# Moving the exactness flag's product forward, a hint on the branch behind it, and a branch body without GpSimd DMAs

## The chip, the cores and the metric

The kernel runs on one core of one Trainium2 chip. The metric is device time in microseconds. It includes a little of what lies around the program, so it is slightly longer than the span from the program's first recorded instruction to its last.

## What is computed

The input is eight images of 384 channels and 32 x 32 pixels. Two blocks follow each other, in float32.

```python
# block 0: a transformer layer on the 1024 tokens of each image
xn = layernorm(xf, g1, beta1)
q, k, v = split(einsum('bnc,oc->bno', xn, w_qkv) + b_qkv)      # 8 heads of 48
attn = softmax(einsum('bhnd,bhmd->bhnm', q, k) * SCALE)
x1 = einsum('bnc,oc->bno', heads(attn @ v), w_proj) + b_proj + xf
h = gelu(einsum('bnc,oc->bno', layernorm(x1, g2, beta2), w_fc1) + b_fc1)
y = x1 + einsum('bnh,oh->bno', h, w_fc2) + b_fc2
# block 1: a convolution block with a global response norm
z = depthwise_conv7x7(y, dw_w) + dw_b
h = gelu((layernorm(z) * ln_w + ln_b) @ w1 + b1)              # 384 -> 1536
gx = sqrt(sum(h * h, pixels)); nx = gx / (mean(gx, channels) + eps)
out = y + (gamma * (h * nx) + beta + h) @ w2 + b2              # 1536 -> 384
```

## The kernel before, in words

The whole work is unrolled over the images in a function `main()` (L1500 to 1671). Channels lie on the 128 partitions, in three groups; pixels lie along the free dimension. TensorE does the products of image b while VectorE does the depthwise convolution of another image, ScalarE the exponentials and gelus, and GpSimd some adding DMAs. The order of the instructions on each engine is the order in which the code issues them (`tc.manual_schedule`, L1674). Chains of VectorE and ScalarE work are woven in between products by a small planner, `Flow`, which adds up estimated TensorE time and steps a chain when its time has come. [...]

The softmax of `main()` does not subtract a row maximum. So the kernel has a second way of computing everything, `exact_path()` (L1677 to 1700), which does subtract it, in a loop over the images. Which way counts is decided from the smallest and largest sum of exponentials, `low` and `high`, which `rest()` inside `attention` updates for each image:

- L1704 to 1706: `fine` is 1 on each partition where `low` and `high` lie within bounds. Three VectorE instructions. They stand behind `main()` in the code, but not under its fixed order, and the trace has them at 2903 us, during the attention of the last image.
- L1708: a product with a matrix of ones adds `fine` over the partitions into a PSUM tile `n_fine`.
- L1710: VectorE compares the sum with 127.5 and writes `again`, an integer.
- L1712: `values_load` makes every one of the five engines read `again` from SBUF into a register.
- L1713: every engine compares and branches. With the inputs used here `again` is 0, and the exact path is skipped.

In the program as built, the body of the exact path stands between the branch and the block that is jumped to. On GpSimd some 90 instructions lie in between, on SP 230, on ScalarE 580, on VectorE 700 and on TensorE 5,100. The block that is jumped to has only bookkeeping: each engine raises its semaphores by as much as the exact path would have raised them. ScalarE, VectorE and TensorE do that in one instruction each, SP in eight (one for each DMA semaphore). GpSimd does it in one, `INC_SWDGE_SEM`, for the eight semaphores of its own DMAs, behind four waits. Then follows the end of the program (under L1800): twelve waits of SP for all semaphores, and two barriers, in which every engine drains, reports, and is released by GpSimd.

The last work of `main()` is the product with w2 of the last image, `grn_down_straight` (L1110 to 1140): nine blocks of 12 products each (L1130), each followed by one VectorE addition (L1138) and one output DMA on SP's queue (L1139). Ahead of it stand the last block of the same product for the image before (L1668) and the end of `grn_scale` (L1669), which has a small product with ones of its own (`gxsum`, L1188) and scales the first weights of w2.

Of the kernel before, what the change touches and what calls it, by code (L numbers as in the profile page):

```python
# [46 lines left out]
F32 = mybir.dt.float32  # L47
AF = mybir.ActivationFunctionType
ALU = mybir.AluOpType
AX = mybir.AxisListType  # L50

P = 128
# [99 lines left out]
def block_kernel(  # L152
# [13 lines left out]
    nc = tc.nc  # L166
# [10 lines left out]
    ps_o = ctx.enter_context(tc.tile_pool(name="ps_o", bufs=4, space=PSUM))  # L177
    flow = Flow()
    quiet = []
    s_fc2 = dram.tile([P, len(FORMS), 4 * P], F32, tag="s_fc2", bufs=1, name="s_fc2")  # L180
    s_w2 = dram.tile([P, len(FORMS), 4 * P], F32, tag="s_w2", bufs=1, name="s_w2")
    s_qk = dram.tile([P, CT, 4 * P], F32, tag="s_qk", bufs=1, name="s_qk")
# [52 lines left out]
    def o_tile(name):  # L235
        return ps_o.tile([P, NH], F32, tag="o", name=name)
# [551 lines left out]

    def difference(dst, more, less):

        nc.scalar.mul(dst, less, -1.0)
        nc.gpsimd.dma_start(out=dst, in_=more, accum_op=ALU.add)

# [34 lines left out]
    def by_thirds(xt, hid, e, made, weights, wname, column, done, name):  # L828

        b11, b12, b21, b22, b31, b32 = (
            [hid[:, 4 * k + 2 * i : 4 * k + 2 * i + 2, half(n)] for i in range(2)] for k in range(3) for n in range(2)
        )
        c11, c12, c21, c22, c31, c32 = (xt[:, r, half(n)] for r in range(CT) for n in range(2))
        spare = three.tile([P, 2, NH], F32, tag="p", name=f"{name}_spare")
        count = iter(range(len(FORMS)))

        def product(pairs):  # L840
            n = next(count)
            if n % 2:
                bank = ps_s.tile([P, 2, NH], F32, tag="s", name=f"{name}_p{n}")[:, 0, :]
            else:
                bank = o_tile(f"{name}_p{n}")
            w = weights.at(wname, n)
            accumulate(bank, [(w[:, k, :], pairs[k // 2][:, k % 2, :]) for k in range(4)])
            weights.used(wname, n)
            return bank

        def copy(dst, bank):
            nc.scalar.copy(dst, bank)
            return dst

        def temporary(key):
            return two.tile([P, NH], F32, tag="r", name=f"{name}_{key}")

        def bias(r, dst, part):
            nc.vector.scalar_tensor_tensor(dst, part, column(r), dst, ALU.add, ALU.add)

        def op(dst, x, y, which=ALU.add):
            nc.vector.tensor_tensor(dst, x, y, which)  # L862

        def both_pairs(dst, x, y, which=ALU.add):
            for i in range(2):
                op(dst[i], x[i], y[i], which)
                yield 1.6

        def adding(dst, src):
            for i in range(2):  # L870
                nc.gpsimd.dma_start(out=dst[i], in_=src[i], accum_op=ALU.add)

        making_e = None if made else flow.spawn(both_pairs(e, b11, b12, ALU.subtract), paced=True)
        n16 = copy(spare[:, 0, :], product(b12))
        bias(2, c31, product(b21))
        flow.finish(making_e)
        f, h = b21, b11
        making_f = flow.spawn(both_pairs(f, e, b21, ALU.subtract), paced=True)
        making_h = flow.spawn(after(making_f, both_pairs(h, e, b31, ALU.subtract)), paced=True)
        p = product(e)  # L880
        making_e = flow.spawn(after(making_h, both_pairs(e, h, b12)), paced=True)
        op(c31, p, c31)
        op(c21, c21, p, ALU.subtract)
        bias(2, c32, product(b22))
        flow.finish(making_f)
        g = b22
        adding(g, f)
        n17 = copy(spare[:, 1, :], product(f))
        flow.finish(making_h)
        n15 = copy(temporary("n15"), product(h))  # L890
        flow.finish(making_e)
        adding(h, b32)
        p = product(e)
        op(n15, p, n15)
        flow.finish(flow.spawn(both_pairs(f, f, b12)))
        bias(0, c11, p)
        bias(0, c12, n15)
        op(n16, n15, n16)
        op(c32, n16, c32)
        op(n17, n16, n17)  # L900
        op(c31, n17, c31)
        done(2, 0)
        bias(1, c22, product(g))
        adding(g, b32)
        op(c11, product(b31), c11)
        op(n17, product(f), n17, ALU.subtract)
        making_f = flow.spawn(after(None, both_pairs(f, f, g, ALU.subtract)), paced=True)
        d = b31
        making_d = flow.spawn(after(making_f, both_pairs(d, g, b31, ALU.subtract)), paced=True)
        p = product(h)  # L910
        op(c12, p, c12)
        op(c22, c22, p, ALU.subtract)
        op(c32, p, c32)
        done(2, 1)
        n18 = copy(temporary("n18"), product(g))
        flow.finish(making_f)
        p = product(f)
        op(n18, p, n18)
        op(c12, p, c12)
        op(c11, n18, c11)  # L920
        op(n17, n18, n17)
        op(c22, n17, c22)
        done(1, 1)
        bias(1, c21, n17)
        op(c12, product(b32), c12)
        done(0, 1)
        flow.finish(making_d)
        p = product(d)
        op(c11, p, c11)
        done(0, 0)  # L930
        op(c21, p, c21)
        done(1, 0)
# [26 lines left out]
    def keep(b, xt):  # L959

        kept = dram.tile([C, N], F32, tag="kept", name=f"kept_{b}")
        nc.sync.dma_start(out=kept.rearrange("(c p) n -> p c n", p=P), in_=xt)
        return kept
# [475 lines left out]
    def first_values(xn):  # L1439
# [45 lines left out]
        for what in FIRST.split():  # L1485
# [11 lines left out]
            else:  # L1497
                step(what)

    def main():  # L1500
        nc.gpsimd.memset(ones, 1.0)
        nc.gpsimd.memset(eps0, EPS0)
# [105 lines left out]
        for b in range(B):  # L1608
# [6 lines left out]
            if b < B - 1:  # L1615
                mlp(b, xt, xn, weights, b, ln2, rest, lambda: next_norms(b), lambda ln: conv_norm(b, ln))
            else:
                acc = state["acc"]
                mlp_by_halves(b, xt, xn, weights, ln2, rest, last_convolution)
            kept[b] = keep(b, xt)  # L1620
            if b + 1 < B:
                acc = state["acc"]
# [45 lines left out]
        grn_down_straight(*args, f"{B - 2}_b", B - 2, blocks[-1:])  # L1668
        flow.finish(scale)  # L1669
        blocks = [(r, part) for r in range(CT) for part in LAST]  # L1670
        grn_down_straight(B - 1, y_last, kept[B - 1], weights, B - 1, B - 1, blocks)

    engines = {nc.tensor.engine, nc.vector.engine, nc.scalar.engine, nc.gpsimd.engine, nc.sync.engine}
    with tc.manual_schedule(engines=engines):  # L1674
        main()

    def exact_path():  # L1677

        load_wqkv(nc.scalar, nc.scalar)
        with tc.For_i(0, B) as b:  # L1680
            table[0] = None
            weights = Weights(plan_fc1("x") + plan_fc2_fast("x") + plan_w1("x") + plan_w2("x"))
            xn, xt = load_x(b, "xn"), load_x(b, "x")
            flow.finish(both(xn, xn, eps0, "g1", "ln1_x", True))
            values("x", xn)
            qT, kT, last_tile, _ = qk("x", xn)
            last_tile()
            exact_attention(xt, qT, kT)
            xn = one.tile([P, CT, N], F32, tag="xn", name="xn2_x")
            flow.finish(layernorm(xt, xn, 0, eps0, "g2", "ln2_x", True))  # L1690
            ln = layernorm(xt, xn, 1, eps0, "g2", "ln2_x", True)
            mlp("x", xt, xn, weights, "x", ln, None)
            kept = keep("x", xt)
            acc = one.tile([P, CT, N], F32, tag="acc", name="acc_x")
            flow.finish(convolution(acc, 0))
            flow.finish(both(acc, acc, eps1, "lnw", "ln3_x", True))
            flow.finish(block_differences(acc))
            y, gx = grn_up("x", acc, weights, "x")
            flow.finish(grn_scale("x", gx, weights, "x", y))
            grn_down("x", y, load_kept("x", kept), weights, "x", b)  # L1700


    fine = small.tile([P, 2], F32, tag="fine", name="fine")
    nc.vector.tensor_scalar(fine[:, 0:1], low, SUM_LOW, None, ALU.is_ge)  # L1704
    nc.vector.tensor_scalar(fine[:, 1:2], high, SUM_HIGH, None, ALU.is_le)
    nc.vector.tensor_tensor(fine[:, 0:1], fine[:, 0:1], fine[:, 1:2], ALU.mult)
    ps = o_tile("n_fine")
    nc.tensor.matmul(out=ps[:, :1], lhsT=ones, rhs=fine[:, 0:1], start=True, stop=True)  # L1708
    again = small.tile([P, 1], mybir.dt.int32, tag="again", name="again")
    nc.vector.tensor_scalar(again, ps[:, :1], P - 0.5, None, ALU.is_lt)  # L1710
    skip = "a comparison gives 0 or 1"
    seen = nc.values_load(again[0:1, 0:1], min_val=0, max_val=1, skip_runtime_bounds_check_because=skip)  # L1712
    with tc.If(seen > 0):  # L1713
        exact_path()


# [87 lines left out]
```

## Time and profile before

| what | us |
|---|---|
| three runs: median (lowest to highest) | 3299.46 (3298.49 to 3303.13) |
| the profiled execution's own time | 3299.18 |
| its span, first to last instruction | 3297.2 |
| TensorE busy in the span | 3274.5 (99%) |
| VectorE, ScalarE, GpSimd busy | 2392.0, 1604.5, 484.2 |
| span from the last product's start (L1708) to the end | 11.3 |

How to read it: the time outside the span (3299.18 - 3297.2 = 2.0 us) is what the program doesn't record. A "q" behind an engine's name means its instruction queue: branches, waits, register loads and DMA issues, which do not count as busy time. L1713 is line 1713 of the kernel. A group such as "x8: 17/17/17" gives the number of instructions and the shortest, median and longest duration in ns, and after it the start of the first and of the last, in us.

### The profile page before, as it was taken

What the parts mean: (1) busy time and instruction counts of PE and PEld (TensorE: products, weight loads), DVE (VectorE), ACT (ScalarE), POOL (GpSimd) and SP (SyncE); (2) the same over time, 40 slices, a digit from 0 to 9 for tenths busy, and PEclk for the clock granted to TensorE, in tenths of its full rate; (3) what the DMA queues carried; (4) which work ended last, traced back from release to release, by engine and by line L of the source; (5) the groups of instructions that cost most, each with busy time, mean ns of one, the idle gap of its engine ahead of it and who ended that gap; (6) DMA issues with size and microseconds to landing.
All of it is one profiled execution on the core that took longest, in us unless ns stands there. A gap on an engine that the chain in (4) does not pass through costs nothing.

```text
span 3297.2 us, 38818 instructions
## 1 busy us (share of the span) xinstructions
PE 3274.5 (99%) x14330; PEld 1418.3 (43%) x14330; DVE 2392.0 (73%) x3178; ACT 1604.5 (49%) x2194; POOL 484.2 (15%) x569
## 2 busy tenths in 40 slices
PE   9999999999999999999999999999999999999998
PEld 5344444443344433444344443444434444444455
DVE  4445787887857978579786797767876788879840
ACT  3542663447534375353662636526474355623541
POOL 2111210112110121101111022110220112100000
PEclk9999999999999999999999999999999999999999
DMA  5336732657244663537436374273842647333231
GB/s 198 116 107 153 149 61 71 160 115 151 54 105 134 142 124 57 132 105 173 86 58 146 103 182 76 53 168 92 183 73 58 179 92 172 69 79 89 69 96 43
DMA packets 199110, 368.74 MB, mean 112 GB/s; under 512 B 40768, under 2 KB 46784, under 8 KB 198528
## 3 DMA queue, kind: packets, MB, share of 16 engines
q0 software_dynamic: 80896, 158.63, 26.4%
q1 hardware_dynamic: 117728, 206.83, 20.8%
q8 instruction: 116, 1.90, 0.2%
q10 hardware_dynamic: 288, 0.71, 0.1%
q14 instruction: 82, 0.67, 0.1%
HBM read 187.03 MB, written 34.60 MB: 67 GB/s over the span
## 4 chain that ended last, share of the span: by engine, by line
PE 98%; DVE 1%; DMA 1%; ACT 0%; issue 0%; POOL 0%; SPq 0%; DVEq 0%; POOLq 0%; ACTq 0%
PE fc L351 17%; PE s L670 13%; PE o L690 13%; PE h L358 10%; PE fc_p L358 10%; PE o_p L358 9%; PE qk L358 6%; PE v L590 4%; PE o L1130 4%; PE proj L612 4%; PE h_last L1174 2%; PE h L338 2%; PE qk L338 1%; PE ln_sum L394 1%; PE ln_var L394 1%; PE ln_var L380 0%
## 5 line engine op out<-in xcount | busy, mean ns | idle before, releaser
L1004 DVE SCALAR_TENSOR_TENSOR acc<-pad,vec,acc 128x870 f32<-128x870 f32 (+7 forms) x861 | 963.3, 1154 | 9.1 <-DMA acc<-tap 4.5
L679 ACT ACTIVATE p<-s 128x1024 f32<-128x1024 f32 x512 | 524.0, 1024 | 283.6 <-PE s L670 276.6
L670 PE MATMUL s<-qk 48*64 48x512 f32 x4096 | 541.5, 592 | 0.2 <-ACT qk L505 0.2
L690 PE MATMUL o<-p,v 64*64 64x512 f32 x4096 | 537.7, 589 | 0.0
L351 PE MATMUL fc<-xn,fc 128*128 128x512 f32 x1152 | 502.3, 594 | 0.0
L1026 POOL DMA_DIRECT2D acc<-tap x294 | 253.5, 884 | 1208.9 <-ACT tap L1025 751.4
L351 PEld LDWEIGHTS fc<-xn,fc 128*128 128x128 f32 x1152 | 217.5, 190 | 280.6 <-issue 269.3
L358 PE MATMUL fc_p<-hid,fc 128*128 128x512 f32 x728 | 317.7, 593 | 0.0
L370 ACT ACTIVATE hid<-fc,bfc_f 128x512 f32<-128x512 f32 x192 | 131.3, 686 | 344.3 <-PE fc L351 344.2
L690 PEld LDWEIGHTS o<-p,v 64*64 64x64 f32 x4096 | 163.5, 133 | 278.4 <-issue 270.2
L670 PEld LDWEIGHTS s<-qk 48*64 48x64 f32 x4096 | 159.7, 133 | 277.2 <-issue 221.8
L358 PE MATMUL o_p<-y,w 128*128 128x512 f32 x624 | 270.9, 592 | 0.0
L1075 DVE TENSOR_TENSOR y<-h,y 128x512 f32<-128x512 f32 x288 | 196.7, 689 | 90.0 <-PE h L358 75.4
L1025 ACT ACTIVATE tap<-pad,vec 128x512 f32<-128x512 f32 x294 | 213.0, 734 | 18.6 <-DMA acc<-tap 18.4
L358 PEld LDWEIGHTS fc_p<-hid,fc 128*128 128x128 f32 x728 | 137.7, 190 | 176.5 <-issue 172.4
L358 PE MATMUL h<-acc,w_A 128*128 128x512 f32 x432 | 207.2, 595 | 0.0
L358 PEld LDWEIGHTS o_p<-y,w 128*128 128x128 f32 x624 | 118.0, 190 | 148.7 <-issue 132.0
L1004 DVE SCALAR_TENSOR_TENSOR wqkv<-pad,vec,wqkv 128x377 f32<-128x377 f32 (+24 forms) x288 | 177.2, 684 | 0.6
L631 DVE TENSOR_TENSOR attn<-o,attn 128x512 f32<-128x512 f32 x64 | 44.1, 689 | 166.9 <-ACT attn L629 166.9
L796 ACT COPY pad<-x 128x512 f32<-128x512 f32 x48 | 30.2, 635 | 247.6 <-DVE x L862 191.7
L549 DVE TENSOR_TENSOR qk<-qk,qk 128x512 f32<-128x512 f32 x168 | 114.3, 688 | 37.4 <-PE qk L358 26.9
L612 PE MATMUL proj<-attn,wproj_sb 128*128 128x512 f32 x288 | 127.3, 595 | 0.5 <-DVE attn L657 0.5
(334 smaller groups left out, 3754.2 us busy)
## 6 DMA issues: line engine op xcount, KB each, us to landing
acc<-tap POOLq DMA_DIRECT2D x294, 256.0 KB, 3.5
w_A<-in_w SPq DMA_DIRECT2D x72, 384.0 KB
fc<-s_fc SPq DMA_DIRECT2D x91, 256.0 KB
hid<-hid POOLq DMA_DIRECT2D x42, 512.0 KB, 6.9
fc<-in_wfc SPq DMA_DIRECT2D x54, 384.0 KB
w<-s_w SPq DMA_DIRECT2D x78, 256.0 KB
y<-y POOLq DMA_DIRECT2D x36, 512.0 KB, 7.0
kept<-x SPq DMA_DIRECT2D x8, 1536.0 KB
```

Source lines behind the costliest of these rows:

```text
L351: nc.tensor.matmul(out=ps, lhsT=lhsT(k), rhs=rhs(k)[:, half(h)], start=(k == 0), stop=(k == nk - 1))
L358: nc.tensor.matmul(out=bank, lhsT=lhsT, rhs=rhs, start=k == 0, stop=k == len(pairs) - 1)
L590: nc.tensor.matmul(out=ps[:, :C], lhsT=xn[:, k, t * P : (t + 1) * P], rhs=wv_sb[:, k, :], start=(k == 0), stop=(k == CT - 1),)
L612: nc.tensor.matmul(out=ps, lhsT=wproj_sb[:, m, ct * P : (ct + 1) * P], rhs=attn[:, m, :], start=(m == 0), stop=(m == CT - 1),)
L670: nc.tensor.matmul(out=s[64 * i : 64 * i + 64, j, :], lhsT=kT[64 * j : 64 * j + HD, m, k0 : k0 + 64], rhs=qT[64 * j : 64 * j + HD, m, half ...
L679: nc.scalar.activation(p, s, AF.Exp)
L690: nc.tensor.matmul(out=outs[i][64 * j : 64 * j + 64, :], lhsT=v[keys, t, at : at + 64], rhs=p[keys, j, :], start=(t == 0), stop=(t == KT - 1),
L1004: nc.vector.scalar_tensor_tensor(dst, window, tap, dst, ALU.mult, ALU.add)
L1025: nc.scalar.mul(t.rearrange("p (h w) -> p h w", w=W), window, tap)
L1026: nc.gpsimd.dma_start(out=acc[:, ct, half(h)], in_=t, accum_op=ALU.add)
L1075: nc.vector.tensor_tensor(dst, bank, part, ALU.add)
L1130: nc.tensor.matmul(out=ps, lhsT=tiles[k], rhs=y(k, part), start=(k == 0), stop=(k == HT - 1))
```

## The change

Three things are changed.

1. In `exact_path()` nothing is issued on GpSimd's DMA queue any more: a Python flag `exact[0]` is set while it is recorded, and then `difference` and `adding`, which make two differences and twelve sums by adding DMAs for each image, use VectorE instructions instead. `main()` is recorded before the flag is set and is not touched by that.
2. The flag is computed inside `main()`: `fine` behind the MLP of the last image, the product with ones and `again` directly ahead of the last image's `grn_down_straight`. What is left behind `main()` is the register load and the branch.
3. The branch gets a label, and a hint "LikelyTaken" for it is placed ahead of `main()` on all five engines. In the built program it is one instruction on each engine, behind the entry barrier and ahead of everything else of `main()`; it names the branch. The jump over the exact path is the branch's taken side.

```diff
+    exact = [False]
...
     def difference(dst, more, less):
 
+        if exact[0]:
+            nc.vector.tensor_tensor(dst, more, less, ALU.subtract)
+            return
         nc.scalar.mul(dst, less, -1.0)
         nc.gpsimd.dma_start(out=dst, in_=more, accum_op=ALU.add)
...
         def adding(dst, src):
             for i in range(2):
-                nc.gpsimd.dma_start(out=dst[i], in_=src[i], accum_op=ALU.add)
+                if exact[0]:
+                    op(dst[i], dst[i], src[i])
+                else:
+                    nc.gpsimd.dma_start(out=dst[i], in_=src[i], accum_op=ALU.add)
...
+    def whether_fine():
+
+        fine = small.tile([P, 2], F32, tag="fine", name="fine")
+        nc.vector.tensor_scalar(fine[:, 0:1], low, SUM_LOW, None, ALU.is_ge)
+        nc.vector.tensor_scalar(fine[:, 1:2], high, SUM_HIGH, None, ALU.is_le)
+        nc.vector.tensor_tensor(fine[:, 0:1], fine[:, 0:1], fine[:, 1:2], ALU.mult)
+        return fine
+
+    def whether_again(fine):
+
+        ps = o_tile("n_fine")
+        nc.tensor.matmul(out=ps[:, :1], lhsT=ones, rhs=fine[:, 0:1], start=True, stop=True)
+        again = small.tile([P, 1], mybir.dt.int32, tag="again", name="again")
+        nc.vector.tensor_scalar(again, ps[:, :1], P - 0.5, None, ALU.is_lt)
+        return again
...
                 mlp_by_halves(b, xt, xn, weights, ln2, rest, last_convolution)
+                fine = whether_fine()
...
         blocks = [(r, part) for r in range(CT) for part in LAST]
+        again = whether_again(fine)
         grn_down_straight(B - 1, y_last, kept[B - 1], weights, B - 1, B - 1, blocks)
+        return again
 
+    tc.mark_branch_hint_location("exact", "LikelyTaken", engines)
     with tc.manual_schedule(engines=engines):
-        main()
+        again = main()
 
     def exact_path():
 
+        exact[0] = True
...
-    fine = small.tile([P, 2], F32, tag="fine", name="fine")
-    nc.vector.tensor_scalar(fine[:, 0:1], low, SUM_LOW, None, ALU.is_ge)
-    nc.vector.tensor_scalar(fine[:, 1:2], high, SUM_HIGH, None, ALU.is_le)
-    nc.vector.tensor_tensor(fine[:, 0:1], fine[:, 0:1], fine[:, 1:2], ALU.mult)
-    ps = o_tile("n_fine")
-    nc.tensor.matmul(out=ps[:, :1], lhsT=ones, rhs=fine[:, 0:1], start=True, stop=True)
-    again = small.tile([P, 1], mybir.dt.int32, tag="again", name="again")
-    nc.vector.tensor_scalar(again, ps[:, :1], P - 0.5, None, ALU.is_lt)
     skip = "a comparison gives 0 or 1"
     seen = nc.values_load(again[0:1, 0:1], min_val=0, max_val=1, skip_runtime_bounds_check_because=skip)
-    with tc.If(seen > 0):
+    with tc.If(seen > 0, label="exact"):
         exact_path()
```

More of the change, by code (lines that the diff above doesn't have):

```diff
@@ L1498, in first_values @@
                 step(what)
+    def whether_fine():
[10 more added lines that the diff above has]
+        return again
+    engines = {nc.tensor.engine, nc.vector.engine, nc.scalar.engine, nc.gpsimd.engine, nc.sync.engine}
     def main():
@@ L1670, in main @@
         blocks = [(r, part) for r in range(CT) for part in LAST]
+        again = whether_again(fine)
         grn_down_straight(B - 1, y_last, kept[B - 1], weights, B - 1, B - 1, blocks)
-    engines = {nc.tensor.engine, nc.vector.engine, nc.scalar.engine, nc.gpsimd.engine, nc.sync.engine}
+        return again
+    tc.mark_branch_hint_location("exact", "LikelyTaken", engines)
     with tc.manual_schedule(engines=engines):
-        main()
+        again = main()
     def exact_path():
+        exact[0] = True
         load_wqkv(nc.scalar, nc.scalar)
```

## The prediction

> **What bounds the kernel now.** I read the page first, then the chain of work that ended last, then what each engine did behind the last product.
>
> ```profile
> span 3297.2 us, 38818 instructions
> ...
> PE 3274.5 (99%) x14330; PEld 1418.3 (43%) x14330; DVE 2392.0 (73%) x3178; ACT 1604.5 (49%) x2194; POOL 484.2 (15%) x569
> ...
> q8 instruction: 116, 1.90, 0.2%
> ...
> q14 instruction: 82, 0.67, 0.1%
> ...
> PE 98%; DVE 1%; DMA 1%; ACT 0%; issue 0%; POOL 0%; SPq 0%; DVEq 0%; POOLq 0%; ACTq 0%
> ```
>
> TensorE is busy 99% of the span and makes 98% of the chain, and the change leaves its products alone. So only the tail can gain. The two "instruction" queues are the fetches of the program itself: 116 packets of 16.4 KB (1.90 MB / 116) and 82 of 8.2 KB (0.67 MB / 82). The chain in the last 17 us:
>
> ```profile
> 3279.95 6.21 PE o L1130 x23
> 3286.16 0.02 issue
> 3286.18 0.55 DVE res L1138
> 3286.74 0.06 DVE again L1710
> ```
>
> It stops at 3286.8, and the span ends at 3297.2: 10.4 us without any busy engine. The last output DMA is issued on SP at 3286.764 (L1139), and all engines read the flag from 3286.8 to 3287.7 (L1712, 0.46 to 0.54 us each). What follows is in the groups of two lines of the kernel, the branch and the end of the program:
>
> ```profile
> L1713 SPq EVENT_SEMAPHORE  x8: 17/17/17, 3290.9 to 3291.4; - x8
> ...
> L1713 POOLq COMPARE_BRANCH  x1: 45/45/45, 3287.4 to 3287.4; - x1
> L1713 PEldq COMPARE_BRANCH  x1: 3809/3809/3809, 3287.4 to 3287.4; - x1
> L1713 DVEq COMPARE_BRANCH  x1: 72/72/72, 3287.4 to 3287.4; - x1
> L1713 SPq COMPARE_BRANCH  x1: 50/50/50, 3287.8 to 3287.8; - x1
> L1713 POOLq INC_SWDGE_SEM  x1: 1797/1797/1797, 3287.9 to 3287.9; - x1
> L1713 ACTq EVENT_SEMAPHORE  x1: 17/17/17, 3290.7 to 3290.7; - x1
> L1713 DVEq EVENT_SEMAPHORE  x1: 21/21/21, 3290.9 to 3290.9; - x1
> L1713 PEldq EVENT_SEMAPHORE  x1: 51/51/51, 3291.3 to 3291.3; - x1
> ```
>
> ```profile
> L1800 POOLq DRAIN  x3: 51/107/6679, 3289.7 to 3297.0; - x3
> L1800 SPq DRAIN  x3: 7/7/13, 3292.2 to 3296.7; - x3
> L1800 PEldq DRAIN  x2: 8/8/8, 3291.4 to 3296.7; - x2
> L1800 DVEq DRAIN  x2: 10/64/117, 3293.6 to 3296.7; - x2
> ```
>
> Two things are to be seen. First, the jump: PE, ACT, DVE and SP stand 3.1 to 3.8 us between branch and next instruction (SP: 3287.751 to 3290.872), GpSimd only 0.19 (3287.398 to 3287.586). Second, GpSimd: `INC_SWDGE_SEM` takes 1.8 us and the drain behind it 6.68, to 3296.418; all others have drained by 3292.3 (SP) and 3293.7 (DVE) and wait for it. GpSimd's drain sets the end, and 0.83 us of barriers follow (to 3297.247).
>
> [...]packets on the instruction queues at 3288.5 to 3288.8, 1.1 us after the branches, and the engines go on 2.2 us later; GpSimd, whose target is 90 instructions away, goes on at once. [...]here 45 to 72 ns are recorded where no fetch is in it. [...]the last output landed at 3288.573 by its semaphore, 1.81 us after its issue at 3286.764 (the one before: 1.84). [...]
>
> **The change part by part.**
>
> *The exact path without GpSimd DMAs.* The jumped-to block of GpSimd loses its four waits and `INC_SWDGE_SEM`. A drain of GpSimd elsewhere takes 0.05 to 0.19 us (other rows of that group, 0.186 at the entry). Alone, this moves the last drain from 3296.4 to DVE's at 3293.69: 2.7 us. DVE's own drain is late because, between 3290.9 and 3293.6, it waits for a second fetch (packet at 3291.4)[...].
>
> *The flag ahead.* `n_fine` costs PE what `gxsum` costs in the chain, 0.12 us for its two passes, now in front of the last w2 instead of behind it: +0.12. Its operands are old by then. On DVE `again` (0.146) goes between two additions that lie 7 us apart, and the three instructions of `fine` (0.46 us) move from 2903 to about 3026; the DVE queue waits 3.7, 1.1, 1.3 and 1.5 us for PE later on, so they cost nothing; without that cover they would cost 0.5. Behind the last product no engine waits for `again` any more. GpSimd, which has no work in the last stretch, and ACT, whose last activation ends at 3230.7, take their branch some 55 us before the end: load, fetch, `INC_SWDGE_SEM` and drain would all be hidden there. So for GpSimd the first two edits remove the same stall; it counts once. PE and DVE come to the branch at about 3286.6 and 3286.9 instead of 3287.4. SP doesn't: its register load stood behind the last DMA's issue already. What is queued behind SP's load is only the end.
>
> *The hint.* It adds one instruction to each engine ahead of everything. On SP it stands before the first load of x, with which the chain begins. No hint runs in the trace before. Its cost there lies between 0 and 0.2 us: register moves at the entry stand 0.07 us apart on SP; I take 0.07. Its gain lies between nothing and the whole stall, down to GpSimd's 0.19 us: SP 2.9 us. I take the whole; the stalls of PE (to 3290.6 then) and DVE (3290.4) matter only if they stay.
>
> *The sum, hint working.* Last output issued at 3286.764 + 0.07 + 0.12 = 3286.95; landed 1.81 later, 3288.76. SP has jumped at 3288.15 and stands at the second of its eight waits, for this DMA. From there to its drain's report it took 3290.967 to 3292.297 = 1.33 us: 3290.09, with 0.02 to wake up 3290.11. PE, DVE, ACT and GpSimd are long there. Barriers 0.83: 3290.94. That is 6.3 us less than 3297.247. The profiled execution took 3299.18, so 3292.9; the median of the runs is 0.28 higher: **3293.2**. The new last wait is SP's, for the output, and its row of semaphore instructions.
>
> **The rivals.**
>
> *A, the hint works on every engine: 3293.2.* [...]Its own range is 3292.0 to 3294.6: both small shifts may be 0 (-0.2), start and product dearer (+0.4), a wait in DVE's or PE's jump may remain in part, and the three runs before spread by some us.
>
> *B, the hint does nothing at its branch*[...]. SP stalls as before: 3292.297 + 0.19 for its report, 0.02, 0.83: 3293.34, a gain of 3.9: 3295.5. PE and DVE are done by 3290.7. For it: nothing in the profile shows a hint that survives fetches.
>
> *C, the hint fetches at once* [...]one extra stall of 2.2 to 3.8 us on PE or SP in the first 30 us, where PE has no slack: 3293.2 + 3.3 = 3296.5.
>
> *D, slower: [...]* PE crosses some 114 blocks of 16.4 KB. If each crossing fetched the jump's target in place of the next block, it would cost about 2.2 us each, 250 us: 3543. It decides from (6.3 + 6.6) / 114 = 0.11 us for each block on. Against it: a block lasts PE some 29 us and a fetch of one takes 0.9 to 1.0[...].
>
> *The change may also not do what it says:* the 6.7 us may be GpSimd's drain itself and not `INC_SWDGE_SEM`. The time would be A's all the same, since the drain then lies at 3225.
>
> **How the numbers follow.** A 0.70, B 0.20, C 0.04, D 0.06. The measurement of this kernel tells 0.2% (6.6 us, below 3292.86 or above 3306.1) from no change. A lies 0.3 us on the near side of the lower bound, less than its unknowns; I split it 0.38 below and 0.32 above, leaning lower because the last output no longer lands among four fetches. So faster 0.38, same 0.32 + 0.20 + 0.04 = 0.56, slower 0.06. The range goes from 3291.0 (A's lower end and a median 1 us low) to 3296.8 (B and most of C); D and the far end of each case are left out.
>
> **What would show it.** The register loads of GpSimd and ACT at 3225 and 3231; no `INC_SWDGE_SEM` at the end; branch to next instruction 0.2 us on PE, DVE and SP (A) or 3.1 to 3.8 (B); a packet on the instruction queues for each target long before 3286 (A) or 1.1 us after the branch (B); SP's drain last, near 3290.1. C would show as a gap on PE within the first 30 us, D as a gap on PE at each packet of q8. I would be wrong if another engine than SP reports last, or if the time outside the span isn't 2.0 us any more.

## The result and the profile after

| | before | changed |
|---|---|---|
| median of 22 runs each, us | 3299.98 | 3295.64 |
| ratio, 95% interval | | 0.9986, 0.998 to 0.9993 |
| the profiled execution's own time | 3299.18 | 3294.61 |
| its span | 3297.2 | 3292.8 |
| last output's DMA issued on SP | 3286.76 | 3288.60 |
| from there to the end of the span (the tail) | 10.48 | 4.23 |

The kernel is 4.3 us faster by the medians, and 2.3 to 6.6 us by the interval (0.0007 and 0.002 of 3300): a real gain, but one within 0.2%. Two runs of the changed kernel, of 3437.91 and 18366.36 us, stand apart from its other twenty and are not in the ratio.

The page of the changed kernel, its lines for the span, the engines, the instruction queues and the chain:

```profile
span 3292.8 us, 38818 instructions
...
PE 3275.4 (99%) x14330; PEld 1415.7 (43%) x14330; DVE 2393.0 (73%) x3178; ACT 1605.6 (49%) x2194; POOL 484.5 (15%) x569
...
q8 instruction: 115, 1.88, 0.2%
...
q14 instruction: 77, 0.63, 0.1%
...
PE 89%; DVE 1%; DMA 0%; issue 0%; ACT 0%; SPq 0%; POOL 0%; DVEq 0%; POOLq 0%
```

The engines do what they did before. The instruction queues carry one packet less (q8, 115 for 116) and five less (q14, 77 for 82). That PE's share of the chain is 89% and not 98% says nothing of the kernel: here the chain is followed back only to 308.5 us. Its last pieces, in order of time (start, us, what):

```profile
3274.66 13.34 PE o L1137 x51
3288.00 0.03 issue
3288.03 0.55 DVE res L1145
```

As before, the chain stops with the last addition; `again` is no longer behind it. Next the two lines of the kernel that made the tail before. First the branch (now L1734), as groups of instructions:

```profile
L1734 SPq EVENT_SEMAPHORE  x8: 17/17/17, 3290.1 to 3291.1; - x8
L1734 POOLq COMPARE_BRANCH  x1: 65/65/65, 3227.2 to 3227.2; - x1
L1734 ACTq COMPARE_BRANCH  x1: 68/68/68, 3229.4 to 3229.4; - x1
L1734 ACTq EVENT_SEMAPHORE  x1: 17/17/17, 3232.3 to 3232.3; - x1
L1734 PEldq COMPARE_BRANCH  x1: 504/504/504, 3283.6 to 3283.6; - x1
L1734 PEldq EVENT_SEMAPHORE  x1: 51/51/51, 3288.0 to 3288.0; - x1
L1734 DVEq COMPARE_BRANCH  x1: 84/84/84, 3288.6 to 3288.6; - x1
L1734 DVEq EVENT_SEMAPHORE  x1: 21/21/21, 3289.2 to 3289.2; - x1
L1734 SPq COMPARE_BRANCH  x1: 70/70/70, 3289.6 to 3289.6; - x1
```

GpSimd and ACT branch 66 and 63 us before the end. (ACT's queue goes on 2.9 us after its branch, although it has the hint: until 3232.29 its own last activations run, which stand ahead of the branch in the code.) VectorE and SP go on 0.59 and 0.51 us after their branch (3288.649 to 3289.237, 3289.595 to 3290.109), where it was over 3 us. PE's branch itself takes 0.504 us, where it took 3.809; it comes 5.0 us ahead of the last output's issue, and PE's products go on beside it. `INC_SWDGE_SEM` is gone. Then the end of the program (L1821), which has the entry's hints as well:

```profile
L1821 POOLq DRAIN  x3: 51/103/6685, 3227.4 to 3292.6; - x3
L1821 SPq DRAIN  x3: 7/7/13, 3291.9 to 3292.3; - x3
...
L1821 PEldq DRAIN  x2: 8/8/8, 3288.2 to 3292.3; - x2
L1821 DVEq DRAIN  x2: 10/14/17, 3289.3 to 3292.3; - x2
...
L1821 SPq BRANCH_PREFETCH_HINT  x1: 56/56/56, 0.8 to 0.8; - x1
```

The line to read is the first. GpSimd's long drain is still there, with 6,685 ns, and it begins at 3227.4, with no `INC_SWDGE_SEM` ahead of it. It was not removed, it was moved under PE's work. SP drains last now, at 3291.9; DVE has drained 2.6 us before.

### The profile page after: what moved, and what is told of

Read it like the earlier page. It is cut to its first block, busy times and chain, and to the rows that moved or that the text cites. A ratio compares the mean times of both kernels' runs of the same rounds, so it can differ in the third digit from the quotient of the medians.

```text
span 3292.8 us, 38818 instructions
## 1 busy us (share of the span) xinstructions
PE 3275.4 (99%) x14330; PEld 1415.7 (43%) x14330; DVE 2393.0 (73%) x3178; ACT 1605.6 (49%) x2194; POOL 484.5 (15%) x569
## 4 chain that ended last, share of the span: by engine, by line
PE 89%; DVE 1%; DMA 0%; issue 0%; ACT 0%; SPq 0%; POOL 0%; DVEq 0%; POOLq 0%
PE fc L352 15%; PE s L671 12%; PE o L691 12%; PE h L359 10%; PE fc_p L359 10%; PE o_p L359 9%; PE qk L359 6%; PE o L1137 4%; PE v L591 3%; PE proj L613 3%; PE h_last L1181 2%; PE h L339 2%; PE ln_var L395 1%; PE ln_sum L395 1%; PE ln_var L381 0%; PE ln_sum L381 0%
## 5 line engine op out<-in xcount | busy, mean ns | idle before, releaser
L1082 DVE TENSOR_TENSOR y<-h,y 128x512 f32<-128x512 f32 x288 | 197.0, 690 | 89.8 <-PE h L359 75.2
```

Source lines behind the costliest of these rows:

```text
L1082: nc.vector.tensor_tensor(dst, bank, part, ALU.add)
```

## Experiments

The tail, from the issue of the last output's DMA to the end, is what the change works on, and it is read from one trace to some 0.1 us. From lowest to highest, the two named above left out, the runs of one kernel lie 5 to 11 us apart, so the runs give the sign and the traces the size. Theory **T**: three stalls lay side by side at the end, GpSimd's (`INC_SWDGE_SEM` 1.8 us, drain 6.7 us), VectorE's and SP's (the jump). The time is set by the longest that is left; the flag takes away the first and the hint the others. **R**: GpSimd's drain is long because of `INC_SWDGE_SEM`, so that the exact path without DMAs matters. **U**: the hint costs time along the whole kernel, for the last output was issued 1.84 us later than before.

### The exact path without GpSimd's DMAs, alone

```diff
 def difference(dst, more, less):
+    if exact[0]:
+        nc.vector.tensor_tensor(dst, more, less, ALU.subtract)
+        return
...
-                nc.gpsimd.dma_start(out=dst[i], in_=src[i], accum_op=ALU.add)
+                if exact[0]:
+                    op(dst[i], dst[i], src[i])
+                else:
+                    nc.gpsimd.dma_start(out=dst[i], in_=src[i], accum_op=ALU.add)
```

> Only the exact path without GpSimd's DMAs, no flag ahead, no hint. Theory T (GpSimd's last drain takes 6.7 us by itself, whatever stands ahead of it): INC_SWDGE_SEM is gone from the end of GpSimd's queue, its drain keeps 6.7 us and still comes last, the end moves by the 1.8 us of INC_SWDGE_SEM: 1.8 us faster than before. Rival R (the prediction's first reading: the drain is long because of INC_SWDGE_SEM): the drain takes 0.05 to 0.2 us, VectorE's or SP's drain comes last, 2.7 us faster.

Measured: 3298.26 us against 3300.28, ratio 0.9993 (0.9985 to 1.0002); tail 8.33 us, 2.15 less than before. The end of the program in this kernel (L1808):

```profile
L1808 POOLq DRAIN  x3: 51/107/6679, 3285.0 to 3292.2; - x3
L1808 SPq DRAIN  x3: 7/7/13, 3289.5 to 3291.9; - x3
```

The drain has its 6.68 us without any `INC_SWDGE_SEM`, and SP is done 2 us earlier and waits for it. T holds and R falls. The 2.15 us are the 1.8 of `INC_SWDGE_SEM` and the 0.33 of the waits ahead of it (3287.586 to 3287.912 in before).

### The flag ahead, alone

```diff
+        again = whether_again(fine)
         grn_down_straight(B - 1, y_last, kept[B - 1], weights, B - 1, B - 1, blocks)
```

(with `whether_fine` and `whether_again` as in the change, and neither of the other parts)

> Only the flag ahead of the last image's w2; the exact path keeps GpSimd's DMAs, no hint. T and R: GpSimd branches near 3225 us, INC_SWDGE_SEM (1.8) and the drain (6.7) are over by 3240; PE, VectorE and SP still stand 3 to 3.8 us behind their branch; the end comes 3.3 to 3.9 us earlier than before, less 0.1 for n_fine. Rival U (the hint costs time along the whole kernel): the same 3.3 to 3.9, since there is no hint.

Measured: 3296.95 us, ratio 0.9989 (0.9982 to 0.9996), 3.3 us faster by the medians; tail 6.74 us, 3.74 less. The end of its program (L1819):

```profile
L1819 POOLq DRAIN  x3: 51/107/6679, 3227.3 to 3292.7; - x3
L1819 SPq DRAIN  x3: 7/7/13, 3291.2 to 3292.4; - x3
...
L1819 DVEq DRAIN  x2: 10/64/117, 3292.1 to 3292.5; - x2
```

GpSimd's 8.5 us are hidden, although all of them are still executed (`INC_SWDGE_SEM` at 3225.4, 1.79 us). VectorE drains last: after its jump (3289.6) it stands once more until 3292.1, 2.5 us, as it did in before from 3290.876 to 3293.573, 2.7 us. Packets start on the instruction queues in that time, at 3290.2 and 3290.5 here and at 3291.32 to 3291.50 in before; that VectorE stands for one of them is the author's estimate from these times.

### The hint, alone

```diff
+    tc.mark_branch_hint_location("exact", "LikelyTaken", engines)
     with tc.manual_schedule(engines=engines):
...
-    with tc.If(seen > 0):
+    with tc.If(seen > 0, label="exact"):
```

> Only the hint; flag and exact path as before. T: branch to next instruction falls from 3.1 to 3.8 us to 0.5 or 0.6 on PE, VectorE and SP, but GpSimd's INC_SWDGE_SEM and drain set the end as before: 0 gained, 0.1 us lost at the entry, so 0.0 to 0.2 us slower and not to be told from before. U (the hint costs time along the whole kernel): about 1.8 us slower, with the last output's issue near 3288.6 instead of 3286.8.

Measured: 3300.40 us against 3300.28, ratio 0.9999 (0.9991 to 1.0007); tail 10.56 us, 0.08 more than before. The branch (L1714) and the end (L1801) of this kernel:

```profile
L1714 PEldq COMPARE_BRANCH  x1: 504/504/504, 3287.0 to 3287.0; - x1
...
L1714 POOLq INC_SWDGE_SEM  x1: 1812/1812/1812, 3287.5 to 3287.5; - x1
L1714 PEldq EVENT_SEMAPHORE  x1: 51/51/51, 3287.6 to 3287.6; - x1
L1714 DVEq EVENT_SEMAPHORE  x1: 21/21/21, 3287.6 to 3287.6; - x1
```

```profile
L1801 POOLq DRAIN  x3: 51/103/6685, 3289.4 to 3296.6; - x3
L1801 SPq DRAIN  x3: 7/7/13, 3290.0 to 3296.3; - x3
```

The hint does all that it can, and nothing comes of it: SP drains at 3290.0, and then GpSimd is waited for until 3296.1. As to U, the runs show no slowing, but the upper end of their interval leaves room for 2.3 us, and U's 1.8 lies within that. The last output is issued at 3286.34 here, and not near 3288.6; but this execution spent less time at half clock than that of before, which makes the two hard to compare (told below). U is not borne out, and not excluded.

### Flag and hint, the exact path as before

```diff
+    tc.mark_branch_hint_location("exact", "LikelyTaken", engines)
...
+        again = whether_again(fine)
         grn_down_straight(B - 1, y_last, kept[B - 1], weights, B - 1, B - 1, blocks)
...
-    with tc.If(seen > 0):
+    with tc.If(seen > 0, label="exact"):
```

> Flag ahead and hint, the exact path keeps GpSimd's DMAs. T: as the changed kernel, since INC_SWDGE_SEM and drain lie at 3225 to 3235 us, under PE's work: 4.3 us faster than before by the runs, 6.2 us in the tail from the last output's issue to the end. Rival (the path without DMAs is needed for the gain): INC_SWDGE_SEM or a drain near the end again, at least 1.8 us less gained.

Measured: 3294.33 us, ratio 0.9983 (0.9975 to 0.999), 5.95 us faster by the medians; tail 4.20 us (the changed kernel: 4.23). GpSimd's branch (L1733) and the end (L1820):

```profile
L1733 POOLq INC_SWDGE_SEM  x1: 1812/1812/1812, 3227.7 to 3227.7; - x1
...
L1820 POOLq DRAIN  x3: 51/103/6685, 3229.5 to 3292.4; - x3
L1820 SPq DRAIN  x3: 7/7/13, 3291.8 to 3292.1; - x3
```

`INC_SWDGE_SEM` and the drain are over by 3236.2, and nobody waits for them. The first part of the change adds nothing to the other two: the tails are 0.03 us apart.

### The changed kernel without the hint

```diff
-    tc.mark_branch_hint_location("exact", "LikelyTaken", engines)
...
-    with tc.If(seen > 0, label="exact"):
+    with tc.If(seen > 0):
```

> The changed kernel without its hint (both other parts stay): the prediction's case B. T: PE, VectorE and SP stand 3 to 3.8 us behind their branch again; as with the flag alone the tail from the last output's issue to the end is 6.7 us, 3.3 to 3.9 us faster than before. Rival (the hint is worth nothing, the flag does it all): as the changed kernel, a tail of 4.2 us.

Measured: 3296.27 us against 3299.46, ratio 0.9991 (0.9984 to 0.9997); tail 5.93 us. So the hint is worth 1.7 us of tail once the flag is ahead. The tail is 0.8 us shorter than with the flag alone, because here VectorE does not stand a second time behind its jump (it drains at 3289.4) and SP comes last, at 3290.99. GpSimd is not in it. The second stand is only in before and in the kernel with the flag alone, the two with the old exact path and no hint on VectorE; what brings it about was not shown.

### The first part and the hint, the flag where it was

```diff
 def difference(dst, more, less):
+    if exact[0]:
+        nc.vector.tensor_tensor(dst, more, less, ALU.subtract)
+        return
...
+    tc.mark_branch_hint_location("exact", "LikelyTaken", engines)
```

(and `adding` and the branch's label as above; the flag is made behind `main()`, as before)

> The exact path without GpSimd's DMAs, and the hint, but the flag behind the last product as before. T (GpSimd's drain of 6.7 us is the floor as long as GpSimd reads the flag at the end): GpSimd branches as in the kernel with the first part alone, its drain comes last, the tail is 8.3 us, 2.1 us less than before, and the hint adds nothing. Rival (the hint takes GpSimd's wait too): a tail of 4.2 to 5 us.

Measured: 3298.61 us against 3300.00, ratio 0.9996 (0.9988 to 1.0005); tail 8.37 us. The end of the program (L1809):

```profile
L1809 POOLq DRAIN  x3: 51/103/6685, 3288.8 to 3296.0; - x3
L1809 SPq DRAIN  x3: 7/7/13, 3291.0 to 3295.7; - x3
```

GpSimd's drain comes last again, SP has drained by 3291.1. T holds: without the flag ahead the hint is worth nothing.

### The changed kernel once more

The kernel is not altered; the point is the time of the last output's issue.

> The changed kernel once more, unaltered, beside kernels of the same chip. If the missing 1.8 us of the first measurement were spread of the runs, the gain comes out nearer to the 6.2 us by which the tail was shorter (between 4.3 and 6.2, as flag and hint without the third part gave 5.95). If the change costs 1.8 us along the kernel, it stays at 4.3 or below, and the last output is issued 1.8 us later than before again, with the same number of stretches at half clock.

Measured: 3294.79 us against 3299.46, ratio 0.9983 (0.9977 to 0.999); tail 4.29 us. The gain is 5.6 us by the ratio (3.3 to 7.6) and 4.7 us by the medians: the interval holds both the 4.3 us of the first measurement and the 6.2 us of the tail, so the runs do not decide. The last output's issue stands 1.96 us later than in the profile of before again, at 3288.73, with as much time at half clock (17 us in both). That half of the expectation speaks for a cost. The traces of the other kernels help here. They hold stretches of 3.4 us at half clock (between 69.2 and 75.2 us of before, two in a row, the granted clock is 0.50), three to five in each trace up to the last output. In windows of 60 to 80, 125 to 140 and 3160 to 3185 us (us, then busy time of the engines, then the granted clock as the third number from the end), the kernel before and then the first experiment:

```profile
60.00:80.00 20.00, 20.00 (x137) 10.58 (x139) 1.42 (x6) 5.33 (x7) 5.31 (x10) 0.83 0.54 185
...
3160.00:3185.00 25.00, 19.23 (x55) 12.02 (x54) 11.68 (x24) 10.88 (x26) 0.00 (x0) 0.80 0.27 74
```

```profile
60.00:80.00 20.00, 20.00 (x152) 10.22 (x154) 1.41 (x6) 6.46 (x7) 5.31 (x10) 0.91 0.51 185
...
3160.00:3185.00 25.00, 19.24 (x62) 12.82 (x61) 10.09 (x21) 13.02 (x32) 0.00 (x0) 0.86 0.28 78
```

0.83 and 0.80 are two and three stretches (0.17 of 20 us lost is 3.4 us, 0.20 of 25 us is 5.0, so 1.7 for each), 0.91 and 0.86 one and two, and the first experiment's last issue is at 3284.17. But PE is busy all of the first window and only 19.2 us of the last, and a stretch less there brought the six kernels with one less only 1.0 to 1.3 us. So the times of the issue cannot be set right by a count of stretches. They need not be: between 145 and 3160 us all eleven traces run at full clock. Before and the changed kernel there:

```profile
145.00:3160.00 3015.00, 3012.45 (x13019) 1273.14 (x13018) 2308.20 (x2990) 1494.11 (x1983) 447.96 (x502) 1.00 0.48 111
```

```profile
145.00:3160.00 3015.00, 3011.23 (x13014) 1269.50 (x13015) 2307.20 (x2988) 1495.31 (x1984) 448.12 (x502) 1.00 0.48 111
```

PE, the first number behind the comma, is idle 2.6 us there in before and 3.8 in the changed kernel. For the same products it takes 1.61 us more (1.65 in this second run). Against before, the three other kernels without a hint take 0.3 to 0.6 us more, those with all engines hinted 0.6 (the hint alone), 1.5 (flag and hint), 1.8 (first part and hint) and 0.2 less (row end, told below), and the one with the hint on SP alone 1.4 more. So some 0.3 to 0.6 us are the luck of the one profile of before. The other 1 us or so stands in five of seven traces with a hint and in none of four without one. That speaks for a cost of the hint along the kernel, against which the hint alone and the row end speak; one trace for each kernel does not settle it.

### Was the run of 18366 us the exact path?

```diff
-SUM_LOW, SUM_HIGH = 1e-25, 1e25
+SUM_LOW, SUM_HIGH = 1e25, 1e25
```

> The bound for the sums is set so that the flag always asks for the exact path: after the fast path the whole of it is executed again. The output is computed by the exact path. T: the branch is not taken, the engines go on in sequence, and the span grows by the exact path's length. If that makes it about 18,365 us, the one run of the changed kernel at 18,366 us had executed the exact path; if it is some thousand us away from that, that run was something else.

Measured: 10159.77 us, in one run. The exact path takes some 6,865 us on top, not 15,070. The run at 18366 us was not that; what it was stays open.

This trace says something of GpSimd's drain as well. Here GpSimd goes on into the exact path, whose loop (L1709) has drains of its own, and reaches the end of the program (L1821) only at 10153 us:

```profile
L1709 POOLq DRAIN  x14: 34/34/6685, 3227.7 to 9296.0; - x14
L1821 POOLq DRAIN  x3: 34/34/103, 10153.3 to 10157.7; - x3
```

The first drain behind `main()`, at 3227.7, takes 6,685 ns; the thirteen that follow it in the loop take 34 to 44, and the one at the end takes 34. So the 6.7 us do not belong to the end of a program. They belong to the first drain that follows `main()`, in which GpSimd issues 548 DMAs; in this exact path it issues none. The last of these DMAs was issued at 2976.5, some 250 us earlier. What makes that drain long was not shown.

### The hint on SP alone

```diff
-    tc.mark_branch_hint_location("exact", "LikelyTaken", engines)
+    tc.mark_branch_hint_location("exact", "LikelyTaken", {nc.sync.engine})
```

> The changed kernel with the hint on SP alone; PE, ACT, VectorE and GpSimd have none. T (SP's jump and the last output's landing set the end): PE branches beside its last products and VectorE, with a stall of 3.3 us after its branch 0.1 us behind the last addition, drains about 3.4 us after that branch, some 0.1 us later to 0.3 us earlier than SP at its drain; the tail is 4.2 to 4.5 us, as of the changed kernel. Rival (VectorE's jump takes a second fetch, as it did before and with the flag alone): VectorE drains last, tail 6 to 7 us, as without any hint.

Measured: 3294.52 us against 3300.00, ratio 0.9983 (0.9976 to 0.999); tail 5.14 us. That is neither of the two forecasts. VectorE drains early enough (3289.3), so the rival is wrong, and SP drains last, but at 3290.1, 4.3 us behind the last issue and not 3.4. Its row of waits (L1734) and the last issue (L1146):

```profile
L1734 SPq EVENT_SEMAPHORE  x8: 17/17/17, 3287.3 to 3289.3; - x8
```

```profile
L1146 SPq DMA_DIRECT2D out_y<-res x15: 333/338/343, 3123.9 to 3285.8; - x15
```

SP has jumped by 3287.3 and then stands before its second wait, for the output. Of that DMA's sixteen reports to the semaphore fifteen had come by 3287.64, 1.82 us after the issue; the last came at 3288.80, 2.98 after it. From there to the end of SP's drain it is 1.35 us, as in the changed kernel (3290.65 to 3292.006). So this tail is long because the output landed late.

### The last output's wait at the end of SP's row

```diff
-            nc.sync.dma_start(out=image_of(out, index)[r * P : (r + 1) * P, part], in_=res[n])
+            image = image_of(out, index)[r * P : (r + 1) * P, part]
+            pieces = 2 if len(todo) == 9 and n < EXTRA else 1
+            wide = (part.stop - part.start) // pieces
+            for i in range(pieces):
+                nc.sync.dma_start(out=image[:, i * wide : (i + 1) * wide], in_=res[n][:, i * wide : (i + 1) * wide])
```

(`EXTRA` is 6; six more DMAs shift the last output from the second to the eighth of the eight semaphores that SP's DMAs use in turn: 100, 101, 103 to 107 and 110 in before's trace)

> The changed kernel with six of the last image's nine outputs stored in two pieces each, so that the last output's semaphore is the last of SP's eight waits and not the second. T (the end is the landing of the last output and then SP's row of semaphore instructions): of the 1.33 us from landing to SP's drain six waits of 0.07 us go, the tail falls from 4.2 to 3.8 us; by the runs it is 0.4 us faster than the changed kernel, which is below what the runs tell apart. Rival: the row is fetched late and not executed late, and the tail stays at 4.2.

Measured: 3294.36 us, ratio 0.9984 (0.9977 to 0.9991); tail 3.83 us. From the landing (3290.22) to the end of SP's drain it takes 0.90 us where it took 1.35. T holds to 0.1 us. This has the shortest tail of all; by the runs it cannot be told from the changed kernel (0.9983 and 0.9986).

### The traces together

| kernel | ratio, 95% interval | tail, us | drains last |
|---|---|---|---|
| before | | 10.48 | GpSimd |
| hint | 0.9999 (0.9991, 1.0007) | 10.56 | GpSimd |
| first part and hint | 0.9996 (0.9988, 1.0005) | 8.37 | GpSimd |
| first part | 0.9993 (0.9985, 1.0002) | 8.33 | GpSimd |
| flag | 0.9989 (0.9982, 0.9996) | 6.74 | VectorE |
| first part and flag | 0.9991 (0.9984, 0.9997) | 5.93 | SP |
| all, hint on SP only | 0.9983 (0.9976, 0.999) | 5.14 | SP |
| all three | 0.9986 and 0.9983 | 4.23, 4.29 | SP |
| flag and hint | 0.9983 (0.9975, 0.999) | 4.20 | SP |
| all three, wait at the row's end | 0.9984 (0.9977, 0.9991) | 3.83 | SP |

The gains do not add. Alone, flag and hint bring 3.74 and -0.08 us; together 6.28.

## Why the prediction was right, and where it was not

The forecast was 3293.2 us with "same" (within 0.2%) as the likeliest class. The runs gave 3295.64, within the range and within 0.2%, and case A, the working hint, is what the trace shows: SP drains last, behind the output's landing. The cases' chances (A 0.70) were the author's estimate. That "same" came out is in part luck. Case A by itself leaned to "faster" (0.38 against 0.32); 3295.64 lies above A's own range, which ends at 3294.6, and beside the 3295.5 of case B, which did not happen. The tail gained what A said, 6.25 us of 6.3. The time came out higher because the last output was issued 1.65 us later than in A's sum, and because the median of before came out 0.5 us higher as well. By its own steps:

- **The bound.** "GpSimd's drain sets the end": right, and shown by the hint alone and by the first part with the hint, where everything else is early and the drain keeps the end.
- **The first part.** "Alone, this moves the last drain from 3296.4 to DVE's at 3293.69: 2.7 us" is the one step whose mechanism failed. It took GpSimd's drain to be short once its DMAs are gone from the exact path, from the 0.05 to 0.19 us of other drains in that group. The first experiment has the drain at 6.68 us without them, so the part alone gives 2.15. The prediction had named this under "may also not do what it says" and had seen that the time stays A's, since the drain then lies under PE's work; it begins at 3227.4 there. The trace of the exact path has it behind `main()` and not at the end; what makes it 6.68 us long was not shown.
- **The flag ahead.** "For GpSimd the first two edits remove the same stall; it counts once": right, flag and hint reach 4.20 us with or without the first part. `n_fine` was put at 0.12 us. PE's products around it stood 1.62 us behind before's ahead of it and 1.84 behind it: 0.22. `fine` and `again` on VectorE cost nothing that can be seen. PE was put at its branch 0.3 us ahead of the last output's issue (3286.6 and 3286.95); it came 5.0 us ahead (3283.59 and 3288.60), so that its jump lies beside its products.
- **The hint at the entry.** 0.07 us expected; SP's first load starts at 0.866 where it was 0.750: 0.116, within the 0 to 0.2 given.
- **The hint at the branch.** "Down to GpSimd's 0.19 us" was too good: 0.51 on SP and 0.59 on VectorE. It costs nothing, for SP is at its second wait at 3290.2 and the output lands at 3290.65. The prediction also asked for packets "for each target long before 3286". Such packets were not shown: q8 has 115 where it had 116 and q14 77 where it had 82, and a packet tells neither its engine nor its address. What the traces show is the tail. In before four packets start at 3288.49 to 3288.80, behind the start of the branches (3287.36 to 3287.75) and ahead of the next instructions of ACT, VectorE, SP and PE (3290.70 to 3291.30). Here the packet nearest to PE's branch (3284.75) starts after that branch is over (3284.10), none starts between VectorE's branch and its next instruction, and one between SP's, at 3290.06, 0.05 us ahead of the next instruction (3290.109). D did not happen: neither the packet counts nor the spans show any cost of the kind; that the 114 blocks are all PE's was the author's estimate.
- **The landing.** 1.81 us expected, 2.05 measured, of which the first fifteen reports had come by 1.85. "The last output no longer lands among four fetches" leaned the chances the wrong way: among the four packets of before (3288.49 to 3288.80) the output had landed in 1.81 us, and here it took 2.05, with one packet, at 3290.06, ahead of the late report. Whether a packet delays a landing was not shown (last section).
- **SP's row and the barriers.** 1.33 and 0.83 expected, 1.33 and 0.83 measured (3290.671 to 3292.006, then to 3292.84).
- **The sum.** From issue to end 3.99 us were expected (3286.95 to 3290.94), 4.23 measured; the difference is the landing. The issue itself came at 3288.60 and not at 3286.95. Of those 1.65 us the two small costs explain 0.15. The other 1.5 arose upstream: 0.45 between 40 and 219 us, 0.33 near 310, and 0.86 near 2111 us, after VectorE had waited 4.00 us and not 2.30 for a DMA (`r`, by the profile) ahead of `attn`, some 10 us earlier. Together these are 1.64, of which 0.14 came back on the way. The change touches none of these places. By the comparison between 145 and 3160 us above, 0.3 to 0.6 us of it are the luck of the one profile of before. Whether the rest, about 1 us, is spread or a cost of the hint can't be settled: five of seven traces with a hint have it, the hint alone has not, and by the runs the hint alone cannot be told from before. By the medians the gains of the four kernels with flag and hint on all engines (4.3, 4.7, 5.1 and 5.95 us) all fall short of what their tails gained (6.2 to 6.7); but so do those of the two with the flag and no hint (3.3 and 3.2 against 3.7 and 4.6). The time outside the span was counted as unchanged and is 0.15 us shorter (1.78 for 1.93).

The chances for case B were fair as to its size: without the hint the tail is 5.93 us, where the prediction's B has 6.39 (3286.95 to 3293.34).

## What to carry to other kernels

When several engines stall side by side at the end of a program, an edit is worth only what the next one in line leaves: look at who drains last, then at who would be last without him, before pricing the edit. A long step of an idle engine (here a 6.7 us drain) need not be made shorter; letting that engine reach it early, by taking its last decision off the end, hides it whole. A sum made from one profile carries that profile's luck: here nine of the ten other traces took 0.3 to 1.8 us longer than that one profile on the same stretch of products at full clock, and 1.65 us is what the sum missed.

## What was not expected of the hardware

- GpSimd's first drain behind `main()` takes 6.68 us in all twelve traces, whether it begins at 3224.6 or at 3289.7 us, with `INC_SWDGE_SEM` ahead of it or not. Where the exact path follows, the drain at the end of the program takes 0.03 us.
- A `BRANCH_PREFETCH_HINT` at the entry is recorded with 45 to 56 ns in the hinted kernels of the table above; given once, 3,290 us ahead, it cut the stall at the branch from 2.6 to 3.8 us to 0.5 or 0.6 us on PE, VectorE and SP, and did not on the engines that had none.
- One of the sixteen reports of the last output's DMA comes late in seven traces. The landing then takes 2.02 to 2.11 us with all engines hinted (four traces) and 2.98 us with VectorE not hinted (three); in the other four kernels of the table it takes 1.81. In the seven, a packet on the instruction queues starts 1.45 to 1.52 us after the output's issue; in the four, the first packet starts 1.53 us after it or later. But the seven are also just the kernels with the flag ahead, and 1.52 and 1.53 lie close together, so the traces do not tell the packet from whatever else the flag moves.
